# Layer 0's bias: sign passes, two more folds and an added row per key in place of the last matrix product

## The chip, the cores and the metric

The kernel runs on one core of a Trainium2 chip. A core has four compute engines that run side by side, each through its own instructions in order: TensorE (PE, matrix products, with a separate row PEld for its weight loads), VectorE (DVE), ScalarE (ACT) and GpSimd (POOL). SyncE (SP) computes nothing here; it issues DMA transfers in order and waits, in its queue, for what they need. All transfers share 16 DMA engines. The metric is the time of one execution on the device in microseconds, the median of three.

## What is computed

Four layers run one after the other on x (2 x 512 x 32 x 32); the change touches layer 0 alone. Layer 0 is an attention with 16 units (2 images x 8 heads). Each unit has 1024 queries and only 64 keys, sampled from the image at learned places. To the similarity comes a bias that is a small network of the distance between a query and a key:

```python
pos = grid_q[:, :, None, :] - grid_kv[:, None, :, :]
bias = jnp.sign(pos) * jnp.log1p(jnp.abs(pos))
bias = jax.nn.relu(bias @ cpb_w1 + cpb_b1)          # 2 -> 128
bias = jax.nn.relu(bias @ cpb_w2 + cpb_b2)          # 128 -> 128
bias = (bias @ cpb_w3 + cpb_b3).reshape(b, GROUPS, H * W, Hd * Wd)
sim = jnp.einsum('bhid,bhjd->bhij', qh, kh) + bias
attn = jax.nn.softmax(sim, axis=-1)
out = jnp.einsum('bhij,bhjd->bhid', attn, vh)
```

It has 128 hidden values for each of 16 x 64 x 1024 pairs of a key and a query, and this network is most of layer 0.

## The kernel before

**Steps.** `layer0` walks over `quads`, (u, o, half): 16 units u, eight groups o of eight keys, two halves of four keys. One such step is "step 2 o + half" of its unit, 0 to 15. For each step `first_hidden` makes h1, the first hidden layer of four keys, on DVE (L726), one step ahead: four 128 x 1024 halves in tiles of which two steps' worth exist. `second_hidden` (from L736) then runs the second layer for the four keys in four quarters q of 32 hidden channels: 32 matrix products of 128 x 32 by 512 columns (L752; each is two records in the trace) into hp, a PSUM tile of 4 keys x 32 channels by 1024 queries. There are three such tiles.

**The last layer without a product.** The magnitudes of `cpb_w3` are folded into the second layer and its channels are sorted by sign, so what is left is a sum of 128 values with signs. ACT does Relu on each quarter (L763) and a sign pass on quarter 0 (L767). Then y1 += y0 is an accumulating DMA from POOL (L772), y3 += y2 a POOL addition (L776), and one step later `join` does y3 += y1 on POOL (L779). In six steps of two units, the `fused` ones, DVE does Relu and y3 += y2 in one instruction (L761) and POOL's L776 is left out.

**Folds.** The 32 rows of a key are then folded on themselves by accumulating DMAs from POOL: 128 to 64 rows in `join` (L782), to 32 and to 16 in `refold` (L804, L807), 256 KB and 128 KB at the last two. Two DMAs on SP (L811) then gather the 16 rows of each half, four a key, into `sum` tiles: 128 rows for 32 keys. A tuple in `self.refolds` says when: the folds at the joins of steps i + 2 and i + 3, the gather at the end of step i + 4. `refold_more` works through that list.

**Last product.** In the next unit, at the end of step 5, `sum_product` (L819) adds the four rows of each key, with their signs, into `sim` (PSUM, one bank) by four products with a signed 0/1 matrix, `thrice`. `attend` for unit v = u - 1 follows: keys by queries into the same `sim` (L845), then softmax on DVE and ACT, one part a step, and the products with the values.

**Tables.** The logs of the distances come from DRAM: `table` has a 512 KB load (lb, on SP, L478) for every two groups, called at the start of an odd-numbered step. `send` ties it behind the last gather issued so far (`self.gathered`), in SP's order. POOL makes the table tx from it (L666), tied behind the last addition or fold issued (`self.added`), and DVE makes h1 from tx.

**Order.** The order of instructions on PE, ACT, DVE and POOL is as the program is written (`manual_schedule`); SP's is set by a scheduler within the ties above. `front` is a list of generators that prepare the next pair of units (normed input, queries, offsets, logs, sampled keys), `after` one with `attend` and the output projection. Each step takes one part of `after`, and one of `front` if that part said it was small.

Of the kernel before, what the change touches and what calls it, by code (L numbers as in the profile page):

```python
# [11 lines left out]
F32 = mybir.dt.float32  # L12
# [22 lines left out]
    ("cpb_w1", 2), ("cpb_b1", 1), ("cpb_b2", 1), ("cpb_w3", 1), ("cpb_b3", 1),  # L35
    ("index", 1), ("row", 1), ("shares", 4),
    ("gamma1", 1), ("vb1", CT),
# [20 lines left out]
class Net:  # L58
# [40 lines left out]
    def layer0(self):  # L99
# [3 lines left out]
        with ExitStack() as ctx:  # L103
# [45 lines left out]
            with self.tc.manual_schedule(engines=engines):  # L149
# [40 lines left out]
                for i, (u, o, half) in enumerate(quads):  # L190
# [23 lines left out]
                    if half == 1 and not last_set:  # L214
                        self.refolds.append((i + 2, i + (3 if u == last else 4), self.refold(group[-1][2], sums[o % 2], o // 2, u == last)))
                    if half == 1 and o == 2 and u > 0:
                        v = u - 1
                        sims[v] = ps_s.tile([P, HF], F32, tag="sim", name=f"sim{v}")
                        self.sum_product(sims[v], self.thrice, True, before)
                        if v == 8:  # L220
                            self.advance(after, lambda: False)
                            att = [apool.tile([P, N], F32, tag=f"att{t}", name=f"att{v}_{t}") for t in range(CT)]
                        self.advance(front, lambda: "v" in pairs[v // 2])
                        after.append(self.attend(v, pairs[v // 2], sims[v], att, ps))
                        if v % 8 == 7:
# [18 lines left out]
                self.single_product(u, o, 1, group[3][1], sims)  # L244
                sim = sims.pop(u)
                for n, _ in enumerate(self.attend(u, pairs[u // 2], sim, att, None)):
                    for _ in range({0: 5, 6: 1}.get(n, 0)):
                        next(share)
# [25 lines left out]
    def sorted_weights(self, keep):  # L274
# [43 lines left out]
        signed = keep.tile([P, N_SUMS], F32, tag="signed", name="signed")  # L318
        pool.tensor_scalar(signed, self.places[:, P:], c["sign"], 1.0, ALU.mult, ALU.mult)
        self.thrice, at = signed[:, 0:N_THRICE], N_THRICE  # L320
# [17 lines left out]
        nc.scalar.copy(self.magb, small)  # L338
        self.under = keep.tile([P, 1], F32, tag="under", name="under")
        pool.tensor_scalar(self.under, self.magb[:, 3, 0:1], -1.0, 1.0, ALU.mult, ALU.mult)  # L340
        self.flip = keep.tile([P, 1], F32, tag="flip", name="flip")
# [395 lines left out]
    def second_hidden(self, i, u, o, half, h1, one, final, last_set):  # L737
# [5 lines left out]
        vec, pool = nc.vector, nc.gpsimd  # L743
        fused = half == 1 and u > 0 and o in ((1, 3), (1, 2, 5, 6))[u % 2] and not final
        ys = []
        for q in range(4):
            hp = self.ps_h.tile([P, N], F32, tag="ps", name=f"hp_{u}_{o}{half}{q}")
            for h in range(2):
                cut = slice(h * HF, (h + 1) * HF)
                for k in range(4):  # L750
                    rows = slice(32 * k, 32 * k + 32)
                    nc.tensor.matmul(  # L752
                        hp[rows, cut], lhsT=self.l0w2[:, 32 * q : 32 * q + 32], rhs=h1[k][:, cut], start=True, stop=True
                    )
            if q < 3:
                y = self.hid2.tile([P, N], F32, tag=f"h2{q}", bufs=(2, 3, 2)[q], name=f"h2_{u}_{o}{half}{q}")
            else:
                y = one[half]
            ys.append(y)
            if q == 3 and fused:  # L760
                vec.scalar_tensor_tensor(y, hp, self.under, ys[2], ALU.max, ALU.add)  # L761
                continue
            nc.scalar.activation(y, hp, AF.Relu, bias=self.magb[:, q, 0:1])  # L763
            if q == 0 and fused:
                nc.scalar.activation(y, y, AF.Identity, scale=self.flip, bias=self.magb[:, 3, 0:1])
            elif q == 0:
                nc.scalar.activation(y, y, AF.Copy, scale=self.flip)  # L767
            elif q == 1:
                if final:
                    vec.tensor_tensor(y, y, ys[0], ALU.add)  # L770
                else:
                    self.added = pool.dma_start(y, ys[0], accum_op=ALU.add)  # L772
                if self.join:
                    self.join(final, i)
            elif q == 3:
                self.added = (vec if final else pool).tensor_tensor(y, y, ys[2], ALU.add)  # L776
# [11 lines left out]
    def refold_more(self, i, gather=False):  # L788

        going = []  # L790
        for at, last, fold in self.refolds:
            if at <= i and gather == (at == last):
                for _ in fold:
                    going.append((at + 1, last, fold))
                    break
            else:
                going.append((at, last, fold))
        self.refolds = going

    def refold(self, both, to, c, once):  # L800
# [7 lines left out]
        yield  # L808
        n = 4 if once else 8
        for half in range(2):  # L810
            self.gathered = nc.sync.dma_start(to[2 * c + half :: n, :], both[0::n, half, :])  # L811

# [24 lines left out]

    def attend(self, u, m, sim, att, ps):
        nc = self.nc
        g = u % 8  # L840
        rows = slice((g % 2) * DH, (g % 2 + 1) * DH)
        for h in range(2):
            for jj in range(2):
                at = h * NJ + jj * 32
                nc.tensor.matmul(  # L845
                    sim[at : at + 32, :],
                    lhsT=m["k"][:, g % 2, jj * 32 : jj * 32 + 32],
                    rhs=m["q"][:, 1 + 16 * h : 17 + 16 * h, 1 : 1 + W],
                    start=False,
                    stop=True,  # L850
                )
        yield
        t = self.soft.tile([P, 2 * NB, W], F32, tag="t", name=f"t{u}")
# [1217 lines left out]
def _places():  # L2071
# [5 lines left out]
    at = P  # L2077
    for keys, n in ((8, N_THRICE), (4, N_TWICE), (2, N_FOLDED), (1, N_SINGLE)):
        got[p, at + n - 32 + 4 * (p % keys) + p // 32] = 1
        at += n  # L2080
# [3 lines left out]
def _layout(i):  # L2084
# [10 lines left out]
    def over(v):  # L2095
# [12 lines left out]
        "index": np.arange(P, dtype=np.float32).reshape(P, 1),  # L2108
        "row": (np.arange(P) % 32 // 8).astype(np.float32).reshape(P, 1), "shares": over(np.arange(24, 108, 24, dtype=np.float32)),
        "gamma1": over(l1["gamma"]), "vb1": _per_partition(l1["bv"]),  # L2110
# [45 lines left out]
```

## Time and profile before

| | |
|---|---|
| median of three runs | 3213.95 us (3212.49 to 3214.47) |
| the profiled execution | 3214.26 us |
| its span, from first to last instruction | 3212.5 us, 58859 instructions |
| granted TensorE clock | 1.000 |
| layer 0 (until the first product of the block after it) | 0 to 1925.6 us |
| PE / DVE / ACT / POOL busy, share of the span | 99% / 76% / 60% / 73% |

The costliest groups of layer 0, with the count, the busy time in all and the mean of one:

| line, engine | what | count | us | ns each |
|---|---|---|---|---|
| L752 PE | second hidden layer, hp | 16384 | 1781.4 | 592 |
| L726 DVE | h1 | 1028 | 1181.1 | 1212 |
| L763 ACT | Relu | 978 | 1079.8 | 1110 |
| L779 POOL | y3 += y1 | 254 | 767.3 | 3021 |
| L776 POOL | y3 += y2 | 209 | 672.0 | 3215 |
| L772 POOL | issue of y1 += y0 | 255 | 354.6 | 1391 |
| L767 ACT | sign pass of quarter 0 | 210 | 241.8 | 1152 |
| L761 DVE | Relu and y3 += y2 in one | 46 | 59.1 | 1284 |
| L819 PE | last product | 128 | 18.8 | 592 |

A matrix product's mean of 592 ns is longer than its share of the time, since four of them run at once in different columns of the array: 16384 records fill 1781 us. POOL's times include overlap with the DMA instruction ahead of it. "Idle before" and "waited for" count the time an engine stood until the named instruction released it. Times in a timeline are in microseconds from the start of the span.

### The profile page before, as it was taken

The numbers are of one execution on the slowest core, as the hardware profiler recorded it, in microseconds if no ns is written. First come the engines' busy times: TensorE is split into PE (matmuls) and PEld (weight loads), VectorE is DVE, ScalarE is ACT, GpSimd is POOL, SyncE is SP. The second block draws the span as 40 slices with busy tenths as digits, with TensorE's granted clock in tenths as the row PEclk, the third lists the DMA queues.
The fourth block names the chain that finished last, engine by engine and source line by source line (L and its number), as shares of the span: only waits on it lengthen the run. The fifth ranks groups of instructions, "written<-read, shape, count | busy, mean of one in ns | idle before, by whom it ended". The sixth has DMA issues, their size and how long they took to land.

```text
span 3212.5 us, 58859 instructions
## 1 busy us (share of the span) xinstructions
PE 3194.7 (99%) x24068; PEld 1221.5 (38%) x24068; DVE 2425.7 (76%) x2792; ACT 1913.0 (60%) x1986; POOL 2340.5 (73%) x1633
## 2 busy tenths in 40 slices
PE   9999999999999999999999999999999999999999
PEld 4333333323333333333333334444556433455333
DVE  7788888888887677888877766475475689755897
ACT  7877887787786577787887742111221566113662
POOL 7998999999998679989999954342343458534575
PEclk9999999999999999999999999999999999999999
DMA  6888888898888578888888861110000000000001
GB/s 166 169 172 163 163 176 161 170 176 157 170 168 161 114 146 169 170 167 158 170 169 168 166 163 75 40 44 35 1 1 25 16 1 2 15 1 14 1 1 54
DMA packets 94349, 341.90 MB, mean 106 GB/s; under 512 B 18544, under 2 KB 20720, under 8 KB 76976
## 3 DMA queue, kind: packets, MB, share of 16 engines
q0 software_dynamic: 56672, 248.55, 41.9%
q1 hardware_dynamic: 36384, 87.33, 9.1%
q8 instruction: 194, 3.18, 0.4%
q10 hardware_dynamic: 1008, 2.10, 0.2%
q14 instruction: 91, 0.75, 0.1%
HBM read 67.37 MB, written 4.46 MB: 22 GB/s over the span
## 4 chain that ended last, share of the span: by engine, by line
PE 91%; DVE 5%; DMA 1%; POOL 1%; issue 1%; ACT 1%; DVEq 0%; POOLq 0%; ACTq 0%; SPq 0%
PE hp L752 53%; PE s L1692 5%; PE o L1721 5%; PE qk30P L1467 2%; PE qk20P L1467 2%; PE m_7P L976 1%; PE m_5P L976 1%; PE m_3P L976 1%; PE m_2P L976 1%; PE m_0P L976 1%; PE qk31P L1467 1%; PE qk21P L1467 1%; PE m_6P L976 1%; PE m_4P L976 1%; PE m_1P L976 1%; DVE sum L1708 1%
## 5 line engine op out<-in xcount | busy, mean ns | idle before, releaser
L752 PE MATMUL hp<-h,w2s 128*32 128x512 f32 x16384 | 1781.4, 592 | 2.8 <-ACT h L763 2.5
L726 DVE CUSTOM_DVE_ANT_1 h<-tx,bank 128x1024 f32<-128x1024 f32 (+1 forms) x1028 | 1181.1, 1212 | 170.3 <-PE hp L752 108.3
L763 ACT ACTIVATE h<-hp,magb 128x1024 f32<-128x1024 f32 x978 | 1079.8, 1110 | 360.9 <-PE hp L752 337.8
L752 PEld LDWEIGHTS hp<-h,w2s 128*32 128x32 f32 x16384 | 564.9, 110 | 1184.1 <-issue 1106.9
L779 POOL TENSOR_TENSOR h<-h,h 128x1024 f32<-128x1024 f32 x254 | 767.3, 3021 | 7.4 <-DMA h<-h 6.8
L776 POOL TENSOR_TENSOR h<-h,h 128x1024 f32<-128x1024 f32 x209 | 672.0, 3215 | 1.5 <-ACT h L763 1.5
L772 POOL DMA_DIRECT2D h<-h x255 | 354.6, 1391 | 130.5 <-ACT h L763 122.7
L1696 ACT ACTIVATE e<-s 128x1024 f32<-128x1024 f32 x256 | 262.0, 1025 | 181.0 <-PE s L1692 175.1
L1721 PE MATMUL o<-e,v 64*64 64x512 f32 x2048 | 265.3, 589 | 2.2 <-DVE q L1760 2.2
L1692 PE MATMUL s<-q,k 64*64 64x512 f32 x2048 | 266.0, 591 | 0.0
L767 ACT ACTIVATE h<-h,flip 128x1024 f32<-128x1024 f32 x210 | 241.8, 1152 | 6.9
L804 POOL DMA_DIRECT2D h<-h x124 | 197.5, 1593 | 0.2 <-issue 0.2
L1703 POOL TENSOR_TENSOR some<-some,e 128x1024 f32<-128x1024 f32 x64 | 167.7, 2620 | 26.7 <-ACT e L1696 23.9
L1701 POOL TENSOR_TENSOR some<-e,e 128x1024 f32<-128x1024 f32 x32 | 76.1, 2378 | 141.4 <-DVE sum L1710 106.3
L782 POOL DMA_DIRECT2D h<-h x127 | 158.3, 1247 | 4.6 <-issue 2.5
L807 POOL DMA_DIRECT2D h<-h x120 | 138.2, 1152 | 18.9 <-DMA h<-h 18.3
L1708 DVE TENSOR_TENSOR sum<-sum,e 128x1024 f32<-128x1024 f32 x64 | 124.0, 1937 | 29.5 <-ACT e L1696 26.8
L946 POOL TENSOR_TENSOR mlp_w<-mlp_w 128x512 f32<-128x512 f32 x16 | 23.9, 1493 | 160.1 <-DMA mlp_w<-in_mlp_w 114.7
L1721 PEld LDWEIGHTS o<-e,v 64*64 64x64 f32 x2048 | 77.9, 133 | 145.0 <-issue 135.1
L761 DVE SCALAR_TENSOR_TENSOR h<-hp,under,h 128x1024 f32<-128x1024 f32 x46 | 59.1, 1284 | 96.9 <-ACT h L763 70.9
L1692 PEld LDWEIGHTS s<-q,k 64*64 64x64 f32 x2048 | 76.6, 133 | 133.1 <-issue 117.2
L1042 ACT ACTIVATE mh<-mh,cols 128x512 f32<-128x512 f32 x64 | 46.1, 721 | 124.3 <-DVE mh L1060 64.3
(587 smaller groups left out, 3446.1 us busy)
## 6 DMA issues: line engine op xcount, KB each, us to landing
h<-h POOLq DMA_DIRECT2D x382, 512.0 KB, 5.8
lb<-logs SPq DMA_DIRECT2D x63, 512.0 KB, 7.2
h<-h POOLq DMA_DIRECT2D x124, 256.0 KB, 5.0
mlp_w<-in_mlp_w SPq DMA_DIRECT2D x16, 1024.0 KB, 4.8
h<-h POOLq DMA_DIRECT2D x120, 128.0 KB, 3.8
sum<-h SPq DMA_DIRECT2D x240, 64.0 KB, 3.0
x<-in_x SPq DMA_DIRECT2D x8, 512.0 KB, 7.6
qkw<-in_l_qk SPq DMA_DIRECT2D x2, 2048.0 KB, 7.9
```

The source lines that it names most:

```text
L726: self.nc.vector._custom_dve(TENSOR_ADD_SAT, out=h1[r][:, k, cut, :], in0=x[:, 4 * half + 2 * r + k, :].unsqueeze(1).to_broadcast([P, H // ...
L752: nc.tensor.matmul(hp[rows, cut], lhsT=self.l0w2[:, 32 * q : 32 * q + 32], rhs=h1[k][:, cut], start=True, stop=True)
L763: nc.scalar.activation(y, hp, AF.Relu, bias=self.magb[:, q, 0:1])
L767: nc.scalar.activation(y, y, AF.Copy, scale=self.flip)
L772: self.added = pool.dma_start(y, ys[0], accum_op=ALU.add)
L776: self.added = (vec if final else pool).tensor_tensor(y, y, ys[2], ALU.add)
L779: (vec if final else pool).tensor_tensor(z, z, other, ALU.add)
L804: nc.gpsimd.dma_start(both[0::4], both[2::4], accum_op=ALU.add)
L976: self.nc.tensor.matmul(acc[p], lhsT=w[:, a, k, p * P : (p + 1) * P], rhs=right(r, k), start=k == 0, stop=k == 1)
L1692: nc.tensor.matmul(s[halves[c], par, :], lhsT=ks[p][rows, at : at + DH], rhs=qs[p][rows, cut], start=True, stop=True)
L1696: nc.scalar.activation(e, s, AF.Exp, scale=DH**-0.5)
L1721: nc.tensor.matmul(o[halves[par], r, :], lhsT=v[n // 2][rows, n % 2, at : at + DH], rhs=e[rows, par, :], start=(n == 0), stop=(n == NB - 1),)
```

## The change

For units v = 0 to 13 the last product goes. In its place, one unit later:

- at the end of step 3 (for the first of the two sum tiles) and step 5 (for the second), ACT multiplies the sum tile by its signs in place (`last_sign`, one per row);
- `keys_rows` folds the tile twice more by accumulating DMAs from POOL, 128 rows to 64 (256 KB) and to 32 (128 KB), at the joins two and three steps later, and two DMAs on SP copy the 32 rows, one a key, into a tile `rows` of 128 x 512 at the end of that third step;
- keys by queries now start the sum in `sim` (`keys_queries`, still after step 5), and `attend`, which begins at step 10 instead of step 5, adds `rows` to `sim` on DVE.

So that four rows of a key lie side by side, the gathers write 16 adjacent rows instead of every eighth, and `thrice`, still used by unit 14, has another pattern. The tuple of `refolds` has a third number, the step from which the gather may go. The `rows` tile has the tag and the one buffer of `pt`, the turned weights of the softmax.

The fused steps change too. `late` is the old form (Relu and y3 += y2 on DVE), now at o = 1, 2 of even units and o = 1, 2, 3, 4 of odd ones (before: 1, 3 and 1, 2, 5, 6). `early` is new, at o = 0 and 7 of units 1 to 14: Relu of quarter 2 and y2 += y0 in one instruction on DVE, with neither ACT's Relu of quarter 2 nor the DMA y1 += y0.

```diff
@@ layer0, in the loop over quads
                     if half == 1 and not last_set:
-                        self.refolds.append((i + 2, i + (3 if u == last else 4), self.refold(group[-1][2], sums[o % 2], o // 2, u == last)))
-                    if half == 1 and o == 2 and u > 0:
-                        v = u - 1
+                        end = i + (3 if u == last else 4)
+                        self.refolds.append((i + 2, end, end, self.refold(group[-1][2], sums[o % 2], o // 2, u == last)))
+                    v = u - 1
+                    if half == 1 and o in (1, 2) and 0 <= v < last - 1:
+                        z = before[o - 1]
+                        if o == 1:
+                            rows = self.soft.tile([P, HF], F32, tag="pt", name=f"rows{v}")
+                        nc.scalar.activation(z, z, AF.Copy, scale=self.last_sign)
+                        self.refolds.append((i + 2, i + 4, i + 3, self.keys_rows(z, rows, o - 1)))
+                    if half == 1 and o == 2 and v >= 0:
                         sims[v] = ps_s.tile([P, HF], F32, tag="sim", name=f"sim{v}")
-                        self.sum_product(sims[v], self.thrice, True, before)
+                        if v == last - 1:
+                            self.sum_product(sims[v], self.thrice, True, before)
+                        self.advance(front, lambda: "v" in pairs[v // 2])
+                        self.keys_queries(v, pairs[v // 2], sims[v], v < last - 1)
+                    if v >= 0 and (o, half) == ((5, 0) if v < last - 1 else (2, 1)):
...
-                        self.advance(front, lambda: "v" in pairs[v // 2])
-                        after.append(self.attend(v, pairs[v // 2], sims[v], att, ps))
+                        after.append(self.attend(v, pairs[v // 2], sims[v], att, ps, rows if v < last - 1 else None))
@@ second_hidden
-        fused = half == 1 and u > 0 and o in ((1, 3), (1, 2, 5, 6))[u % 2] and not final
+        late = half == 1 and u > 0 and o in ((1, 2), (1, 2, 3, 4))[u % 2]
+        early = half == 1 and 0 < u < 2 * BP - 1 and o in (0, 7)
...
-            if q == 3 and fused:
-                vec.scalar_tensor_tensor(y, hp, self.under, ys[2], ALU.max, ALU.add)
+            if q == 3 and late:
+                vec.scalar_tensor_tensor(y, hp, self.under[:, 1:2], ys[2], ALU.max, ALU.add)
+                continue
+            if q == 2 and early:
+                vec.scalar_tensor_tensor(y, hp, self.under[:, 0:1], ys[0], ALU.max, ALU.add)
                 continue
             nc.scalar.activation(y, hp, AF.Relu, bias=self.magb[:, q, 0:1])
-            if q == 0 and fused:
-                nc.scalar.activation(y, y, AF.Identity, scale=self.flip, bias=self.magb[:, 3, 0:1])
+            if q == 0 and (late or early):
+                at = 3 if late else 2
+                nc.scalar.activation(y, y, AF.Identity, scale=self.flip, bias=self.magb[:, at, 0:1])
...
-                else:
+                elif not early:
                     self.added = pool.dma_start(y, ys[0], accum_op=ALU.add)
@@ refold_more
-        for at, last, fold in self.refolds:
-            if at <= i and gather == (at == last):
+        for at, last, when, fold in self.refolds:
+            if at < last and at <= i and not gather or at == last and when <= i and gather:
@@ refold
-        n = 4 if once else 8
         for half in range(2):
-            self.gathered = nc.sync.dma_start(to[2 * c + half :: n, :], both[0::n, half, :])
+            at = 2 * c + half
+            if once:
+                self.gathered = nc.sync.dma_start(to[at::4, :], both[0::4, half, :])
+            else:
+                self.gathered = nc.sync.dma_start(to[16 * at : 16 * at + 16, :], both[0::8, half, :])
+
+    def keys_rows(self, z, to, jj):
+
+        nc = self.nc
+        nc.gpsimd.dma_start(z[0::2], z[1::2], accum_op=ALU.add)
+        yield
+        nc.gpsimd.dma_start(z[0::4], z[2::4], accum_op=ALU.add)
+        yield
+        for h in range(2):
+            at = h * NJ + jj * 32
+            self.gathered = nc.sync.dma_start(to[at : at + 32, :], z[0::4, h * HF : (h + 1) * HF])
@@ attend
+        if bias is not None:
+            nc.vector.tensor_tensor(sim, sim, bias, ALU.add)
         t = self.soft.tile([P, 2 * NB, W], F32, tag="t", name=f"t{u}")
```

The rest of the diff makes the signs of the sum tiles' rows at the start (a column `last_row`, a few one-column instructions on POOL) and moves keys by queries out of `attend` into `keys_queries`.

More of the change, by code (lines that the diff above doesn't have):

```diff
@@ L35 @@
     ("cpb_w1", 2), ("cpb_b1", 1), ("cpb_b2", 1), ("cpb_w3", 1), ("cpb_b3", 1),
-    ("index", 1), ("row", 1), ("shares", 4),
+    ("index", 1), ("row", 1), ("last_row", 1), ("shares", 4),
     ("gamma1", 1), ("vb1", CT),
@@ L245, in layer0 @@
                 sim = sims.pop(u)
+                self.keys_queries(u, pairs[u // 2], sim, False)
                 for n, _ in enumerate(self.attend(u, pairs[u // 2], sim, att, None)):
@@ L318, in sorted_weights @@
         signed = keep.tile([P, N_SUMS], F32, tag="signed", name="signed")
-        pool.tensor_scalar(signed, self.places[:, P:], c["sign"], 1.0, ALU.mult, ALU.mult)
+        self.last_sign = keep.tile([P, 1], F32, tag="last_sign", name="last_sign")
+        pool.tensor_scalar(self.last_sign, self.col("last_row"), c["groups"], 2.0, ALU.is_lt, ALU.mult)
+        pool.tensor_scalar(self.last_sign, self.last_sign, -1.0, 1.0, ALU.add, ALU.mult)
+        for cut, sign in ((slice(0, N_THRICE), self.last_sign), (slice(N_THRICE, N_SUMS), c["sign"])):
+            pool.tensor_scalar(signed[:, cut], self.places[:, P:][:, cut], sign, 1.0, ALU.mult, ALU.mult)
         self.thrice, at = signed[:, 0:N_THRICE], N_THRICE
@@ L338, in sorted_weights @@
         nc.scalar.copy(self.magb, small)
-        self.under = keep.tile([P, 1], F32, tag="under", name="under")
-        pool.tensor_scalar(self.under, self.magb[:, 3, 0:1], -1.0, 1.0, ALU.mult, ALU.mult)
+        self.under = keep.tile([P, 2], F32, tag="under", name="under")
+        pool.tensor_scalar(self.under, self.magb[:, 2:4, 0], -1.0, 1.0, ALU.mult, ALU.mult)
         self.flip = keep.tile([P, 1], F32, tag="flip", name="flip")
@@ L790, in refold_more @@
         going = []
-        for at, last, fold in self.refolds:
-            if at <= i and gather == (at == last):
+        for at, last, when, fold in self.refolds:
+            if at < last and at <= i and not gather or at == last and when <= i and gather:
                 for _ in fold:
-                    going.append((at + 1, last, fold))
+                    going.append((at + 1, last, when, fold))
                     break
             else:
-                going.append((at, last, fold))
+                going.append((at, last, when, fold))
         self.refolds = going
@@ L836, in single_product, with keys_queries, attend @@
             )
-    def attend(self, u, m, sim, att, ps):
+    def keys_queries(self, u, m, sim, start):
+        for h in range(2):
+            for jj in range(2):
+                at = h * NJ + jj * 32
+                self.nc.tensor.matmul(
+                    sim[at : at + 32, :],
+                    lhsT=m["k"][:, u % 2, jj * 32 : jj * 32 + 32],
+                    rhs=m["q"][:, 1 + 16 * h : 17 + 16 * h, 1 : 1 + W],
+                    start=start,
+                    stop=True,
+                )
+    def attend(self, u, m, sim, att, ps, bias=None):
         nc = self.nc
@@ L841, in attend @@
         rows = slice((g % 2) * DH, (g % 2 + 1) * DH)
[L842 to L852, printed above, removed]
+        if bias is not None:
+            nc.vector.tensor_tensor(sim, sim, bias, ALU.add)
         t = self.soft.tile([P, 2 * NB, W], F32, tag="t", name=f"t{u}")
@@ L2077, in _places @@
     at = P
-    for keys, n in ((8, N_THRICE), (4, N_TWICE), (2, N_FOLDED), (1, N_SINGLE)):
+    got[p, at + p // 4] = 1
+    at += N_THRICE
+    for keys, n in ((4, N_TWICE), (2, N_FOLDED), (1, N_SINGLE)):
         got[p, at + n - 32 + 4 * (p % keys) + p // 32] = 1
@@ L2108, in _layout @@
         "index": np.arange(P, dtype=np.float32).reshape(P, 1),
-        "row": (np.arange(P) % 32 // 8).astype(np.float32).reshape(P, 1), "shares": over(np.arange(24, 108, 24, dtype=np.float32)),
+        "row": (np.arange(P) % 32 // 8).astype(np.float32).reshape(P, 1),
+        "last_row": (np.arange(P) % 4).astype(np.float32).reshape(P, 1), "shares": over(np.arange(24, 108, 24, dtype=np.float32)),
         "gamma1": over(l1["gamma"]), "vb1": _per_partition(l1["bv"]),
```

## The prediction

> **What bounds the kernel now.** I read the page first, then the chain of waits in layer 0, the busy time by window, the waits of each engine, and last the timeline of GpSimd (POOL) and of the SP queue.
>
> The chain of waits, a stretch of unit 4, and the window of about one unit:
> ```profile
> 624.22 13.87 PE hp L752 x128
> 638.09 0.86 PE sim L819 x8
> 638.94 0.86 PE sim L845 x8
> 639.80 41.20 PE hp L752 x384
> ...
> 535.00:649.00 114.00, 114.00 (x1064) 38.94 (x1060) 97.80 (x108) 90.83 (x90) 106.63 (x79) 1.00 0.86 167
> ```
> TensorE (PE) has no gap: a step of 64 hp records takes 13.87/2 = 6.9 us, one after the other. A unit of 16 steps takes about 114.2 us. The columns of the window line are PE, PEld, DVE, ACT, POOL: POOL is at 106.6 of 114, so it is the second bound, close behind. Its waits over 137 to 936 us, seven units:
> ```profile
> POOL h L772 <- ACT h L763: 36.9, 21, 4.2
> POOL h L807 <- DMA h<-h: 10.6, 10, 2.2
> ...
> POOL h L772 <- DMA h<-h: 1.5, 2, 0.8
> ```
> Only the wait for ACT is real slack (POOL has caught up). The same question over 1200 to 1756 us gives 20.9, 6.6 and 6.0. Over these 1355 us the ACT wait comes to 57.8/1355 x 114.2 = 4.9 us a unit.
>
> POOL's timeline, with the SP queue, and the landing times:
> ```profile
> 575.50 3.16 POOL L779 TENSOR_TENSOR h<-h,h 128x1024 f32<-128x1024 f32 x1
> 578.33 1.06 POOL L807 DMA_DIRECT2D h<-h  x1
> 578.96 1.34 POOL L782 DMA_DIRECT2D h<-h  x1
> 579.54 3.19 POOL L776 TENSOR_TENSOR h<-h,h 128x1024 f32<-128x1024 f32 x1
> 581.93 1.53 POOL L666 TENSOR_SCALAR tx<-lb,cols 128x512 f32<-128x512 f32 x1
> ...
> 581.76 16.49 SPq L811 DMA_DIRECT2D sum<-h  x4
> 598.34 0.53 SPq L478 DMA_DIRECT2D lb<-logs  x1
> ...
> lb<-logs SPq DMA_DIRECT2D x63, 512.0 KB, 7.2
> h<-h POOLq DMA_DIRECT2D x120, 128.0 KB, 3.8
> ```
> The shown spans overlap, so I take each end less the end before it: L807 costs POOL 0.73 us (579.39 - 578.66), L782 0.91, L776 2.43, tx 0.73; elsewhere L772 gives 0.84 and L804 0.80. The gather on SP starts 581.76 - 578.33 = 3.4 us after its fold L807, and lb is issued right behind a gather. In the kernel before that costs nothing: the lb of 569.69 is used by the tx of 581.93, 12.2 us later.
>
> One place shows what a late lb does (unit 9 to 10, where logs were made late):
> ```profile
> 1178.88 3.18 POOL L776 TENSOR_TENSOR h<-h,h 128x1024 f32<-128x1024 f32 x1
> 1193.13 0.77 POOL L666 TENSOR_SCALAR tx<-lb,cols 128x512 f32<-128x512 f32 x1 [11.06 <-DMA lb<-logs]
> ...
> 1199.57 1.92 PE L752 MATMUL hp<-h,w2s 128*32 128x512 f32 x16 [2.24 <-ACT h L763]
> ```
> POOL stood 11.06 us behind the tx, everything queued after it (the fold L772, then the sums) was late, ACT could not reuse its tiles, and PE stopped for 2.24 us and then 0.26: POOL can fall some 8 us behind before PE stops.
>
> **What the skill says.** The Trainium skill, "DMA: Bandwidth & Descriptors", section "SWDGE vs HWDGE vs iDMA": accumulating DMAs can be issued from GpSimd alone, whose cores compute the descriptors; the trace agrees (0.7 to 0.9 us of POOL each). The same page, "Two DMAs through the same engine are not ordered": the engine that issues a dependent DMA must wait for the first one's semaphore. SP does so: its L811 rows wait for the folds. "Perfetto Trace Analysis", section "DMA Instruction — SWDGE (GPSIMD)": the shown end is that of descriptor generation, not of the data; hence 3.8 us to landing for an instruction shown as about 1.1.
>
> **The change part by part.**
>
> *Product removed.* 14 units x 0.86 us (the eight sim L819 records) = 12.0 us off PE. Keys by queries stay (0.86 us, only earlier in order).
>
> *ScalarE.* Signs add 2 passes a unit at about 1.15 us (as L767); the two early folds remove two L763 at 1.11. The late ones move to o = 1, 2, so that a sign pass takes the place of a missing Relu: 5 passes a step, as before. Nothing, hidden by 114 - 91 us. The signs need gathers issued two steps before, as the product did.
>
> *VectorE.* Added a unit: 2 x 1.28 us (as L761) and one 128x512 add at 0.69 (as L867), 3.3 us; 97.8 + 3.3 stays under 113. But DVE can make the h1 of step i+2 only after PE ends step i, and needs 4.6 of the 6.9 us. After step 5 of units 2, 4, 6 and 8 the late add (1.28) now stands with the normed input (L539, median 2.35): 1.28 + 2.35 + 4.62 + about 0.2 = 8.4 against 6.9 + 0.86 of PE: 0.7 us x 4 = 2.8 us, if PE is otherwise the bound. In unit 10 this collision goes.
>
> *Front moved.* attend starts five steps later, so the next pair's offsets run ahead: in unit 9 logs come two steps before lb needs them, and the 2.24 + 0.26 = 2.5 us above go.
>
> *GpSimd issues.* Four new folds: 2 x 0.80 (as L804) + 2 x 0.74 (as L807), about 3.2 with the wider ones a little dearer; two L772 go, 1.7. Net +1.5 us a unit. The bytes stay: 2 x 512 KB go, 2 x (256 + 128) and 4 x 64 KB come, so the DMA share stays near 0.86.
>
> *Gather layout.* 16 adjacent rows instead of every eighth: between nothing and a few tenths of their 3.0 us either way; two steps of slack cover it. I take nothing. The sum tiles (three buffers) are held longer, but a buffer is refilled only after the rows left it, by order on SP; the rows tile shares pt's buffer, free since step 15. Nothing.
>
> *SP queue and the new wait: the dear one.* The rows of the second z are issued at the end of step 8 (its "when" is i + 3, the very step of its second fold); the load lb(u,3) is called at the start of step 9 and tied behind the last gather. So SP holds lb until that fold has landed. On POOL, between the fold and the tx of this lb stand only L782 and L776. This holds in the built order of units 1 to 14. From the fold's issue: 3.4 us to the rows, 1.3 for their two issues (gather pairs took 1.1 to 1.7), 7.2 to lb's landing = 11.9. POOL gets to tx after 0.74 + 0.91 + 2.43 = 4.1. It then stands 7.8 us, in every unit, and however late it runs, since both ends hang on the same fold. Behind it stand L772 and all later sums; ACT waits for their tiles, PE for ACT. With lb at its fastest (5.0) the wait is 5.6, at its slowest (9.2) 9.8.
>
> *Sum.* POOL's slack: 4.9, plus 0.5 (L772's own waits for a DMA, 7.5 us in 1355 rounded down) plus 0.6 (my share of L807's waits, 1.5 us a unit, that a new fold in between covers), less 1.5 for issues, less 0.9 because PE's unit gets shorter: 3.6 us. Each unit is thus longer than PE's by 7.8 - 3.6 = 4.2 us. Units 1 and 9 start without a debt (the projection, 28 us of PE alone, now stands at the head of unit 9) and cost 1.5 each, an estimate below the 2.5 of the 11 us wait. 12 x 4.2 + 2 x 1.5 = 53.4; less 12.0 and 2.5: +38.9 us. The profiled execution took 3214.26 (span 3212.5), against a median of 3213.95: 3253.
>
> **Rivals.**
>
> B, the wait is absorbed and PE stays the bound: -12.0 - 2.5 + 2.8 = -11.7, 3203. For it: no gap on PE, one 11 us wait cost only 2.5. Against: it came once, with two late adds behind it to catch up; fourteen of them don't fit in 3.6 us a unit. It decides where the wait at this tx is under 3.6 us; the time equals the one before at (14.5 - 3)/12 + 3.6 = 4.6. With lb never seen under 5.0 us that needs most of the fold's landing hidden too.
>
> C, the wait is there but smaller and POOL has more slack, so that gain and loss nearly cancel: wait 5.6 and slack 4.7 give 12 x 0.9 + 3 - 14.5 = -0.7, 3214. For it: POOL's slack is the softest number here.
>
> D, the wait is real but VectorE becomes late too: after step 10 the add, the transpose and maxima (3.7 us) stand before h1, with 2.05 us of slack a step; if that adds 0.5 us a unit, 3260. It lies inside A's range.
>
> That the change doesn't do what it says I can exclude: the order of instructions has the products gone and the rows added in 14 units.
>
> **How the numbers follow.** A (with D) 0.72, B 0.20, C 0.08. The likeliest is A: 3253. Its own range: wait 5.6, excess 2.0, 24 + 1.5 - 14.5 = +11, 3225; wait 9.8, excess 6.2, 74.4 + 5 - 14.5 = +65, 3279. A measurement tells 0.2% (6.4 us) from no change. To leave out at most 2 in 10 the range must reach B's centre: 3203 to 3280. Slower 0.73 (A and a little of C), same 0.07, faster 0.20.
>
> **What would show it.** Right: POOL's tx waits for DMA lb<-logs 14 times, 5 to 10 us each (14.6 us in all before); PE hp gets idle, mostly behind ACT or DVE, in step 10 to 12 of each unit; sim<-sum only in two units of PE; the idle at 1199 gone. Wrong: those waits under 4 us, or PE still without a gap in units 2 to 8, or the loss found on DVE after L539.

## The result and the profile after

| | before | changed |
|---|---|---|
| median (lowest to highest, runs) | 3213.33 us (3211.27 to 3214.47, 6) | 3291.17 us (3289.57 to 3293.18, 6) |
| span of the profiled execution | 3212.5 us | 3288.3 us |
| ratio, 95% interval | | 1.0243 (1.023 to 1.0256) |

The change makes the kernel 77.8 us slower. The direction was forecast, the size was not: 38.9 us were expected and the range ended at 3280.

The loss lies in layer 0. Take a unit from its keys by queries (after step 5) to those of the next unit; the first interval begins in unit 1. The fourteen intervals, in us, with two kernels of the experiments beside them (x4 does without the product, x8 is the last repaired version):

```
before   115.3 114.1 114.4 114.1 114.4 114.1 115.5 142.6 119.7 117.4 115.5 114.1 115.6 112.3   sum 1639
changed  115.6 122.6 122.6 119.0 120.9 118.7 124.6 146.7 121.0 118.4 121.8 119.3 122.3 122.0   sum 1716
x4       114.4 113.2 113.5 113.3 113.5 113.2 114.7 141.7 120.3 115.8 114.8 113.2 114.7 112.3   sum 1629
x8       114.8 113.4 115.5 114.9 113.1 114.8 114.2 143.4 113.1 117.2 114.9 114.8 114.3 115.6   sum 1634
```

The changed kernel loses in all but the first interval, up to 9.7 us in one. From the page of the changed kernel, the chain and three groups (busy time, mean of one, then the idle time before them and what ended it):

```profile
PE 63%; POOL 16%; DVE 9%; DMA 6%; issue 4%; ACT 1%; SPq 0%; DVEq 0%; POOLq 0%; ACTq 0%
...
L768 PE MATMUL hp<-h,w2s 128*32 128x512 f32 x16384 | 1816.7, 597 | 53.5 <-ACT h L782 47.9
...
L792 POOL DMA_DIRECT2D h<-h x227 | 333.8, 1471 | 73.0 <-ACT h L782 64.6
...
L681 POOL TENSOR_SCALAR tx<-lb,cols 128x512 f32<-128x512 f32 x63 | 78.4, 1245 | 108.9 <-DMA lb<-logs 72.5
```

PE was 91% of the chain and is 63%. It stands 53.5 us ahead of hp (2.8 before). POOL stands 108.9 us ahead of tx (14.6 before), where the prediction put the dear wait. POOL also still stands 64.6 us for ACT: its slack is not used up although it is what is late. A stall is passed on to ACT and PE within a step or two, as shown next; the slack comes at other times, when POOL has caught up and waits for ACT's next result.

One such stall, in unit 4. First SP's queue, then POOL, then ACT, then PE, each from its own timeline of the changed kernel (start, duration, what, and in brackets the idle time before it with what ended that):

```profile
571.25 1.56 SPq L845 DMA_DIRECT2D rows<-sum  x2
572.86 0.58 SPq L493 DMA_DIRECT2D lb<-logs  x1
```
```profile
565.82 1.93 POOL L841 DMA_DIRECT2D sum<-sum  x1
566.42 2.22 POOL L802 DMA_DIRECT2D h<-h  x1
566.99 4.09 POOL L796 TENSOR_TENSOR h<-h,h 128x1024 f32<-128x1024 f32 x1
578.46 0.77 POOL L681 TENSOR_SCALAR tx<-lb,cols 128x512 f32<-128x512 f32 x1 [7.39 <-DVE bank L897]
579.18 0.86 POOL L792 DMA_DIRECT2D h<-h  x1
```
```profile
583.64 1.11 ACT L782 ACTIVATE h<-hp,magb 128x1024 f32<-128x1024 f32 x1 [5.32 <-DMA h<-h]
```
```profile
584.81 15.39 PE L768 MATMUL hp<-h,w2s 128*32 128x512 f32 x128 [2.48 <-ACT h L782]
```

The rows go out 3.5 us after the issue of their fold ends (565.82 + 1.93 = 567.75), the load of logs right behind them, and tx starts 5.6 us after that load's issue. The timeline names a small copy of DVE as the releaser, which is no input of tx; a wait for several semaphores is put down to the last one seen. The load itself landed 5.4 us after its issue, 0.2 us before tx starts, and x1 and x3 below show that it is what POOL stood for. Behind tx stands the transfer y1 += y0 of L792: ACT waits 5.32 us for a tile that it frees, and PE 2.48 us for ACT. So a wait of 7.39 us stopped PE here, where the prediction read from one place of the kernel before that POOL can fall some 8 us behind.

The gap costs PE more than its length. Windows of the changed kernel around it (length, then PE, PEld, DVE, ACT, POOL busy; then granted clock, DMA share, GB/s):

```profile
582.00:585.00 3.00, 0.52 (x5) 0.19 (x8) 3.00 (x4) 1.32 (x2) 3.00 (x3) 0.90 0.76 153
585.00:592.00 7.00, 7.00 (x56) 1.80 (x54) 5.06 (x5) 5.93 (x6) 7.00 (x6) 0.80 0.63 115
592.00:600.00 8.00, 8.00 (x80) 2.05 (x68) 6.24 (x7) 4.42 (x6) 8.00 (x7) 1.00 1.03 215
```

After the gap the clock is 0.80 on the mean of 7 us, and 56 records of products go through where 65 do at full clock (6.9 us a step of 64). The 128 records that took 13.87 us before take 15.39. The Trainium skill, "TensorE: Matmul & The Clock Gate", section 'Part 1: The HAM clock gate (the "warmup" mystery)', says that the clock halves after an idle stretch of about 3.4 us and comes back after a busy one; the trace agrees in kind, in windows of 2 us the clock reads 0.50 just after such a gap, but not in the length: this gap of PE was 2.48 us. Over all windows of 2 us from 137 to 1756 us, PE's busy time times (1 - clock) adds up to 11.9 us in the changed kernel, and to 0 in the kernel before. The clock fell at seven gaps: four stand behind the load (343.41, 584.81, 1068.42 and 1576.77 us), two behind a gather (448.58 and 928.28, see below), one behind DVE (1683.71).

The waits in the same stretch, the changed kernel (us in total, times, longest):

```profile
ACT h L782 <- DMA h<-h: 79.8, 36, 6.8
POOL tx L681 <- DMA lb<-logs: 66.1, 10, 8.6
...
ACT h L782 <- DMA sum<-h: 40.7, 24, 4.5
DVE sampling L604 <- DMA at<-spots: 36.0, 4, 10.5
...
PEld hp L768 <- DVE h L741: 27.9, 50, 1.0
```

The first two belong together, as shown. The next two, ACT for a gather and DVE for the sampling places, are new as well (4.9 us each before) and stood in no sum of the prediction. They were the rivals for what was left.

Both can be seen in unit 3, before its load of logs is issued. SP, then ACT and PE, then DVE:

```profile
434.52 1.13 SPq L845 DMA_DIRECT2D rows<-sum  x2
439.52 1.16 SPq L834 DMA_DIRECT2D sum<-h  x2
441.11 0.65 SPq L493 DMA_DIRECT2D at<-spots  x1
```
```profile
447.41 2.12 ACT L782 ACTIVATE h<-hp,magb 128x1024 f32<-128x1024 f32 x2 [8.73 <-DMA sum<-sum]
448.58 1.08 PE L768 MATMUL hp<-h,w2s 128*32 128x512 f32 x4 [5.90 <-ACT h L782]
```
```profile
447.75 1.22 DVE L604 TENSOR_TENSOR sampling<-at,bank 128x1024 f32<-128x1024 f32 x1 [9.48 <-DMA at<-spots]
```

The rows of the first tile land at 439.45 us, and the gather follows at once. In all 14 units the gather is issued within 0.4 us of that landing. Its second half lands at 447.30, and ACT, which needs the tile that this gather reads, starts 0.1 us later (the fold `sum<-sum` that the timeline names lands only at 448.6). The places are loaded behind the gather, and DVE stands for them. PE stands 12.3 us behind such gathers in four units (3, 5, 7 and 11), of 46.3 us in front of hp in this stretch.

### The profile page after: what moved, and what is told of

It reads as the page before. It is cut to its first block, busy times and chain, and to the rows that moved or that the text cites. A ratio compares the mean times of both kernels' runs of the same rounds, so it can differ in the third digit from the quotient of the medians.

```text
span 3288.3 us, 58784 instructions
## 1 busy us (share of the span) xinstructions
PE 3217.4 (98%) x23956; PEld 1210.3 (37%) x23956; DVE 2470.8 (75%) x2834; ACT 1905.2 (58%) x1985; POOL 2362.1 (72%) x1664
## 4 chain that ended last, share of the span: by engine, by line
PE 63%; POOL 16%; DVE 9%; DMA 6%; issue 4%; ACT 1%; SPq 0%; DVEq 0%; POOLq 0%; ACTq 0%
PE hp L768 26%; POOL h L799 7%; PE s L1730 5%; PE o L1759 5%; DMA h<-h 3%; POOL h L796 3%; DVE h L741 3%; POOL h L792 2%; PE qk20P L1505 1%; PE qk30P L1505 1%; PE m_0P L1014 1%; PE m_7P L1014 1%; PE m_5P L1014 1%; PE m_4P L1014 1%; PE m_2P L1014 1%
## 5 line engine op out<-in xcount | busy, mean ns | idle before, releaser
L768 PE MATMUL hp<-h,w2s 128*32 128x512 f32 x16384 | 1816.7, 597 | 53.5 <-ACT h L782 47.9
L782 ACT ACTIVATE h<-hp,magb 128x1024 f32<-128x1024 f32 x950 | 1043.1, 1108 | 470.9 <-PE hp L768 306.5
L799 POOL TENSOR_TENSOR h<-h,h 128x1024 f32<-128x1024 f32 x254 | 750.5, 2955 | 14.0 <-DMA h<-h 11.8
L796 POOL TENSOR_TENSOR h<-h,h 128x1024 f32<-128x1024 f32 x209 | 661.9, 3167 | 5.1 <-ACT h L782 5.1
L792 POOL DMA_DIRECT2D h<-h x227 | 333.8, 1471 | 73.0 <-ACT h L782 64.6
L787 ACT ACTIVATE h<-h,flip 128x1024 f32<-128x1024 f32 x182 | 209.6, 1152 | 6.0
L1741 POOL TENSOR_TENSOR some<-some,e 128x1024 f32<-128x1024 f32 x64 | 167.6, 2619 | 26.6 <-ACT e L1734 24.1
L802 POOL DMA_DIRECT2D h<-h x127 | 173.1, 1363 | 6.1 <-issue 4.0
L824 POOL DMA_DIRECT2D h<-h x124 | 168.3, 1358 | 7.6 <-DMA h<-h 5.1
L827 POOL DMA_DIRECT2D h<-h x120 | 148.7, 1239 | 17.0 <-DMA h<-h 16.8
L681 POOL TENSOR_SCALAR tx<-lb,cols 128x512 f32<-128x512 f32 x63 | 78.4, 1245 | 108.9 <-DMA lb<-logs 72.5
```

Of the source, the lines that this page charges most:

```text
L768: nc.tensor.matmul(hp[rows, cut], lhsT=self.l0w2[:, 32 * q : 32 * q + 32], rhs=h1[k][:, cut], start=True, stop=True)
L799: (vec if final else pool).tensor_tensor(z, z, other, ALU.add)
L802: pool.dma_start(one[2][0::2], one[2][1::2], accum_op=ALU.add)
L824: nc.gpsimd.dma_start(both[0::4], both[2::4], accum_op=ALU.add)
```

## The experiments

Each run is compared with runs of the kernel before on the same chip, whose medians lay between 3213.09 and 3214.55 us. All kernels but x4, x11 and x14 do the whole computation.

| run | what | median, us | ratio (95%) |
|---|---|---|---|
| x1 | rows of both tiles a step later | 3246.27 | 1.0104 (1.0088 to 1.0121) |
| x2 | rows of the second tile alone later | 3247.04 | 1.0109 (1.0092 to 1.0126) |
| x3 | rows of the first tile alone later | 3288.84 | 1.0235 (1.0218 to 1.0252) |
| x4 | before, without the product | 3200.53 | 0.9962 (0.9948 to 0.9976) |
| x5 | x1 + fourth sum buffer | 3240.42 | 1.0075 (1.0056 to 1.0093) |
| x6 | x5 without early folds | 3247.78 | 1.0105 (1.0084 to 1.0127) |
| x7 | x5 + sampling later | 3234.67 | 1.0077 (1.0059 to 1.0095) |
| x8 | x7 + attend one step later | 3208.43 | 0.9983 (0.9976 to 0.999) |
| x9 | changed + attend one step later | 3290.53 | 1.024 (1.0223 to 1.0257) |
| x10 | x1 + attend one step later | 3236.20 | 1.0064 (1.0048 to 1.0081) |
| x11 | x4 + attend where the change has it | 3201.52 | 0.996 (0.9946 to 0.9974) |
| x12 | x8 with three sum buffers | 3243.05 | 1.0095 (1.0078 to 1.0112) |
| x13 | x8 with the sampling not later | 3219.50 | 1.0021 (1.0014 to 1.0029) |
| x14 | x7 without the add of the rows | 3208.03 | 0.9984 (0.9977 to 0.999) |
| x15 | x7 without early folds | 3243.77 | 1.009 (1.0073 to 1.0107) |

**The load behind the rows: x1, x2, x3.** The edit of x1; x2 has `i + 2 + o` and x3 `i + 5 - o` in its place:

```diff
-                        self.refolds.append((i + 2, i + 4, i + 3, self.keys_rows(z, rows, o - 1)))
+                        self.refolds.append((i + 2, i + 4, i + 4, self.keys_rows(z, rows, o - 1)))
```

> The rows of both sum tiles are issued one step later, at the end of steps 7 and 9 (when is i + 4), so that SP issues the load lb(u,3), and the stores of logs and spots, ahead of the rows that come after them in the program. Theory T1 (the load held behind the rows is the loss): the waits of tx for lb fall from 109 us to under 20 us and the time to 3203 to 3212. Theory T2 (a good part of the loss is the front moved ahead, DVE standing at the sampling for the at load, and the collisions of late adds on DVE): 3225 to 3250, with the waits of DVE for at<-spots still near 36 us. Theory T3 (POOL is simply out of slack with four more issues a unit): over 3230, with PE idle behind ACT and no waits at tx.

> Only the rows of the second sum tile are issued one step later (end of step 9 instead of 8); those of the first stay at the end of step 6. T1: nearly the whole gain of the run with both late, 3205 to 3215, waits at tx gone. T2: the logs and spots of odd units still go behind the rows of the first tile, DVE still stands some 36 us at the sampling, and the time stays 10 to 25 us above the run with both late.

> Only the rows of the first sum tile are issued one step later (end of step 7 instead of 6); those of the second stay at the end of step 8, with lb behind them. T1: no gain, 3283 to 3293, waits at tx still about 109 us. T2: the waits of DVE for at<-spots fall under 10 us and the time by 10 to 25 us, to 3265 to 3282.

With the second tile's rows out of the load's way 44.1 us go (x2), with both 44.9 (x1), with the first alone 2.3 (x3). The idle time ahead of tx falls from 108.9 us to 11.1 (x2) and 4.5 (x1), and stays at 107.7 in x3. So the dear wait of the prediction is real, is tied to the second tile as it said, and taking it away in this manner brings 44 us.

Both T1 and T2 missed in x1 and x2. T1 had the times 30 us and more too low. T2 had x1's time, but not its waits: DVE's wait for the places is 2.3 us in x1, not 36; it is 25.1 in x2, and yet the two take the same time. In x3 it fell to 9.5 us and brought next to nothing, with the load's stall still there. T3, POOL out of slack, fits the times too, but not the trace: with the load out of the way POOL stands for ACT's results as long as before, 110.7 us in x2 against 99.1 over the same stretch.

The gain is a net one, for the edit brings a wait of its own. The rows of the second tile now leave one step ahead of the add instead of two. The add in the changed kernel and in x2, over 137 to 1756 us (busy, mean | idle before):

```profile
L890 DVE TENSOR_TENSOR sim<-sim,rows 128x512 f32<-128x512 f32 x13 | 9.0, 690 | 0.3 <-DMA rows<-sum 0.3
```
```profile
L890 DVE TENSOR_TENSOR sim<-sim,rows 128x512 f32<-128x512 f32 x13 | 9.0, 695 | 11.8 <-DMA rows<-sum 8.3 <-issue 3.5
```

The lost clock, by the sum above, falls with the gaps too: from 11.9 us to 5.0 in x1 and 0 in x2. What the load's wait alone costs these runs do not tell.

**The product: x4.** `sum_product` is called for unit 14 alone, and keys by queries start the sum; the bias of units 0 to 13 is left out.

> The kernel before, with the last product left out for units 0 to 13 and nothing in its place: these units' similarity is without the bias. This is the gain of the removed product by itself. All theories: 14 x 0.86 = 12.0 us, 3201 to 3202. If POOL is already as much of a bound as PE, less: 3204 to 3210.

12.8 us go. Between x1 and x4 45.7 us are left to be explained. In x2, as much is left (46.5), and there PE stands only 4.8 us in front of hp in the stretch, none of it behind the gathers: it is its weight loads that stand for h1, 44.3 us against 9.8 before. So DVE is late.

**Sum buffers: x5, and the early folds: x6.** The fourth buffer needs 4 KB a partition, found by putting small tiles into parts of others:

```diff
-        return self.hid2.tile([P, N], F32, tag="sum", bufs=3, name=name)
+        return self.hid2.tile([P, N], F32, tag="sum", bufs=4, name=name)
...
-        spots = self.fone.tile([P, 2 * NJ, 2], F32, tag="spots", name=f"at{b}{t}")
+        spots = m["at"]
...
-        wx = self.fone.tile([P, 2 * NJ], F32, tag="wx", name=f"wx{b}{t}")
+        more = self.fone.tile([P, N], F32, tag="xn", name=f"wx{b}{t}")
```

x6 has `early = False` beside it.

> The rows of both tiles late, as in x1_rows_late (3246.27 us), and in addition a fourth buffer for the sum tiles (room for it made by putting three small tiles into parts of others, with the same work). Theory T2, the sum buffers: what x1 still loses comes mostly from a sum tile held until its rows are read, so that the gather into the next tile of that tag waits on SP for the rows' transfer and comes late to ScalarE's Relu; then ScalarE's waits for DMA sum<-h (23.4 us over 137 to 1756 us in x1) fall under 6, and the time to 3215, between 3205 and 3228. Theory T3, VectorE's and GpSimd's additions (two more STT, one add, four folds less two a unit): the time stays within 8 us of x1's, 3238 to 3252, with TensorE waiting behind ScalarE all the same.

> x5_late_four without the two early folds of VectorE a unit (steps 1 and 15 go back to GpSimd's accumulating transfer). GpSimd issues two more transfers a unit, 1.7 us, and VectorE does 2.6 us less. If GpSimd is what is short beside the waits (T2), it gets slower than x5, by 5 to 20 us; if VectorE's early folds are what costs (T3), it gets faster than x5 by 5 to 25 us.

ACT's waits for the gathers went as expected (23.4 us to 2.5), but the time fell by 5.9 us only: T2 missed here. T3 in the form "the early folds cost" falls too, since without them it did not get faster (7.4 us slower, with ranges that overlap). The odd units up to 7 stayed long in x5 (117.8 to 121.2), and DVE's timeline of x5 in unit 5 showed why, with h1 standing behind the sampling; SP's queue is put ahead of it:

```profile
664.88 2.97 SPq L848 DMA_DIRECT2D rows<-sum  x2
667.95 0.98 SPq L494 DMA_DIRECT2D sampling<-spots  x1
```
```profile
675.46 1.22 DVE L605 TENSOR_TENSOR sampling<-sampling,bank 128x1024 f32<-128x1024 f32 x1 [8.11 <-DMA sampling<-spots]
```

Before, the places were loaded at 666.97 us and used at 686.85, 20 us later, because attend's steps came in between. Attend now begins five steps later, and load and use are neighbours. That alone does not make DVE stand: in x11 below, attend begins as late, the places are loaded at 651.51 us and used at 656.92, and DVE stood 0.03 us. In x5 the load goes out right behind the rows, when DVE has already been standing for 0.6 us. How much of the delay is the rows and how much the place of the load in the program was not told apart.

**The sampling: x7, and attend's place: x8.**

```diff
         xnT = m["xT"]
         yield
+        if bt:
+            yield
```
```diff
-                    if v >= 0 and (o, half) == ((5, 0) if v < last - 1 else (2, 1)):
+                    if v >= 0 and (o, half) == ((5, 1) if v < last - 1 else (2, 1)):
```

> x5_late_four (3240.42 us) with one idle turn more between the load of the sampling places and VectorE's first use of them, so that the use comes one to two steps later, behind the late fold of step 11. Theory T4, the front moved: with attend five steps later, the next pair's places are stored, loaded and used within two steps (20 us apart before), VectorE stands up to 8.1 us for them in the odd units, h1 is late and TensorE waits; then the intervals of the odd units (117.8 to 121.3 us in x5) fall to 117 or less, and the time to 3222, between 3212 and 3232. Theory T3, VectorE is simply too full there: the odd units stay within 1 us of x5 and the time between 3234 and 3246.

> x7_sampled_later with attend, which begins with VectorE's add of the rows, one step later (after step 11 in place of step 10). Theory T5: VectorE waits for the second tile's rows at the add (13.6 us in seven units of x5), because the rows are issued only one step ahead; then that wait goes under 3 us and the time falls 6 to 14 us below x7. If the add's wait lies in slack that VectorE has anyway, the time stays within 5 us of x7.

x7 lies 5.8 us under x5, with ranges that overlap (3231.59 to 3244.49 and 3233.46 to 3245.49): not resolved as such, outside T4's 3212 to 3232 and just inside T3's range. The odd units did come down, to between 116.1 and 117.3 in units 1 to 7. x8 falls by 26.2 us, twice what T5 expected, and is faster than the kernel before, by 0.17%. The group of the add, from x7 and then from x8 over 137 to 1756 us (busy, mean | idle before):

```profile
L895 DVE TENSOR_TENSOR sim<-sim,rows 128x512 f32<-128x512 f32 x13 | 9.1, 697 | 15.6 <-issue 9.2 <-DMA rows<-sum 6.3
```
```profile
L895 DVE TENSOR_TENSOR sim<-sim,rows 128x512 f32<-128x512 f32 x14 | 9.7, 692 | 0.0
```

Of the 15.6 us the trace puts 6.3 down to the rows; for 9.2 it shows no releaser. And the waits of PE's weight loads for h1 in the two, x7 and then x8:

```profile
PEld hp L773 <- DVE h L746: 39.8, 72, 1.0
```
```profile
PEld hp L773 <- DVE h L746: 19.2, 47, 1.0
```

A step later the rows have landed, DVE does not stand at the add, and PE waits half as long for h1. Attend's six steps are where DVE has least to spare: in x7 it is busy for 29.8 of 31.0 us from 798.5, with PE at four and a half steps in that time. What it loses there it can hardly make up.

**What adds up and what does not: x9, x10, x11.**

> The changed kernel with one edit: attend and its add of the rows begin one step later (after step 11). The load of logs stays behind the second tile's rows. If the two costs add (load 44 us, attend's place 26 us), 3265, between 3255 and 3275; if the load's stall covers the other, it stays at 3291 within 8 us.

> x1_rows_late (3246.27 us; both tiles' rows a step later) with attend one step later, three buffers for the sum tiles and the sampling as in the changed kernel. If attend's place is what costs (T5, 26 us from x7 to x8), 3220, between 3212 and 3228; what is left against x8 (3208.43 us) is the price of the third buffer and the early sampling. If x8's gain needs the fourth buffer and the later sampling, it stays above 3232.

> x4_before_no_product (3200.53 us; the bias of units 0 to 13 left out) with attend five steps later and the late folds at o = 1, 2 or 1 to 4, as the change places them, and nothing else of the change: no signs, no rows, no new folds, no early folds. It is left out: the bias of units 0 to 13. If attend's place with the sampling two steps behind its load is dear by itself, 3200.5 + 20 to 35, that is 3220 to 3235; if it costs only together with the rows, the add and the early folds of VectorE, 3198 to 3208.

In x9 the same edit that gave 26 us to x7 gives 0.6. The expectation put that down to the load's stall, which is still there (111.1 us ahead of tx); but the changed kernel also has no wait at the add to lose, 0.3 us as shown, and these runs do not tell the two reasons apart. In x10 the edit gives 10.1, a miss against 3220; at 3236.20 it lies where x8's gain was said to need the fourth buffer and the later sampling. x11 (bias of units 0 to 13 left out) has the two moves of the change in the kernel x4 and nothing else of it:

```diff
-                        after.append(self.attend(v, pairs[v // 2], sims[v], att, ps))
+                        going = self.attend(v, pairs[v // 2], sims[v], att, ps)
+                        if v < last - 1:
+                            next(going)
+                    if u > 0 and (o, half) == ((5, 0) if u < last else (2, 1)):
+                        after.append(going)
...
-        fused = half == 1 and u > 0 and o in ((1, 3), (1, 2, 5, 6))[u % 2] and not final
+        fused = half == 1 and u > 0 and o in ((1, 2), (1, 2, 3, 4))[u % 2] and not final
```

It shows that attend's new place, with the late folds moved, costs next to nothing by itself, 1.0 us. It takes unit 9's interval from 120.3 to 113.4, the gain that the prediction claimed from earlier logs, and the other thirteen intervals lose 4.9 us together. The place is dear only with the rows.

**One taken from x8, or from x7: x12 to x15.** Each undoes one edit: `bufs=3`; the idle turn gone; the add of `bias` gone; `early = False`.

> x8_attend_later (3208.43 us) with three buffers for the sum tiles in place of four, nothing else. Theory T2: a sum tile is held until its rows are read, so that the gather into the next one waits on SP, ScalarE's Relu waits for its tile and TensorE for ScalarE (x10, with three buffers: 49.3 us of ScalarE waiting for DMA sum<-h); then this one loses 20 to 30 us and comes to 3233, between 3226 and 3242. If the buffer is worth the 6 us that x1 to x5 showed, 3210 to 3219.

> x8_attend_later without the idle turn between the load of the sampling places and their use (so x5_late_four with attend one step later). Theory T4 (VectorE stands for the places in the odd units): 3214 to 3222; if the later attend already took that wait away, within 4 us of x8, 3204 to 3213.

> x7_sampled_later (3234.67 us) without VectorE's add of the rows, so the bias of units 0 to 13 is left out; the rows are still moved. Theory T5a, the add and its wait for the rows are what makes VectorE late after step 10 (the burst of attend stands ahead of h1): 3212, between 3206 and 3220. Theory T5b, the two early folds of VectorE beside attend are: stays above 3226.

> x7_sampled_later (3234.67 us) without the two early folds of VectorE a unit (their sums go back to GpSimd's transfers). T5b: VectorE gets 2.6 us a unit back around attend, and the time falls to 3215 to 3226. T5a, or GpSimd too short of time: it stays above 3230 or rises, as from x5 to x6 (+7).

x12 is the clear one: three buffers instead of four cost 34.6 us, some more than the 20 to 30 expected. Its memory layout is that of x8, so it is the buffer. SP's queue of x12 in unit 3, then ACT, then PE:

```profile
429.78 1.80 SPq L850 DMA_DIRECT2D rows<-sum  x2
431.68 1.29 SPq L494 DMA_DIRECT2D sampling<-spots  x1
433.02 0.54 SPq L494 DMA_DIRECT2D lb<-logs  x1
435.36 10.66 SPq L839 DMA_DIRECT2D sum<-h  x4
```
```profile
442.94 2.12 ACT L787 ACTIVATE h<-hp,magb 128x1024 f32<-128x1024 f32 x2 [9.83 <-DMA sum<-h]
```
```profile
444.11 16.15 PE L773 MATMUL hp<-h,w2s 128*32 128x512 f32 x135 [7.00 <-ACT h L787]
```

And SP's queue of x8 at the same place:

```profile
424.63 1.46 SPq L839 DMA_DIRECT2D sum<-h  x2
426.26 2.91 SPq L850 DMA_DIRECT2D rows<-sum  x2
429.27 1.03 SPq L494 DMA_DIRECT2D sampling<-spots  x1
430.35 1.35 SPq L494 DMA_DIRECT2D lb<-logs  x1
```

With four buffers the gather goes ahead of the rows. With three it goes into the very tile that the rows are still read from, so it stands behind them and two loads, and is issued 0.15 us after they land (435.21). It also frees the tile that ACT writes next, so ACT stands 9.83 us and PE 7.00. SP is not among the engines whose order the kernel writes out (`engines` of `manual_schedule` has PE, ACT, DVE and POOL): its order follows from what a transfer must wait for, and a buffer less turned it round.

Where the sampling is not later, the fourth buffer is worth less: from x10 to x13, which differ in it and in the small tiles moved for it, 16.7 us. So its price is 5.9, 16.7 or 34.6 us, by what else is in the way. All three have the first tile's rows a step later than the changed kernel has them; there the same order stands in SP's queue (unit 3 above), but a fourth buffer was not tried.

x13: the later sampling is worth 11.1 us in x8 (T4, inside its 3214 to 3222). x14, with the bias of units 0 to 13 left out: without the add x7 falls by 26.6 us, which is about the add's busy and idle time in x7, 9.1 + 15.6 = 24.7 (T5a). x15: without the early folds x7 gets no faster (9.1 us slower, with ranges that overlap), so T5b falls.

## Why the prediction was right in direction and wrong in size

The sum was -12.0 - 2.5 + 53.4 = +38.9 us. Measured, it is -12.8 + 44.9 + 45.7 = +77.8: the product (x4), the load (x1), and what is left between x1 and x4. The step that failed is the one that put this last term at nothing, in three places: VectorE, the front, the sum tiles.

- *Product removed, 12.0.* Right: 12.8 (x4).
- *The dear wait.* Right in place and cause. The unit 4 wait was 7.39 us against 7.8, and the whole 108.9 us in 17 waits is 6.4 on the mean. Its cost was put at 53.4, and 44 to 45 go in x1 and x2. That the two are close is in part luck: the 44 are net of the wait that the edit brings to the add, and have lost clock in them that the prediction did not count.
- *VectorE.* Rival D was named, but given 0.5 us a unit, 7 in all, and kept inside A. Once the load is out of the way DVE is what is late (x2). From x7 to x8 26.2 us go, and the add with its wait costs 26.6/14 = 1.9 us a unit in x7 (x14). The average load, 97.8 of 114, hid that attend's six steps have almost no slack. The wait at the add itself is not the change's: it is 0.3 us there, and came with the later rows.
- *"Front moved"*, taken as a gain of 2.5 alone. The gain came in its place (6.9 us in unit 9's interval, x4 to x11) but not in the sum (x11 is 1.0 us slower than x4). And the places for the sampling came to lie next to their use, behind the rows on SP: DVE stood 36.0 us for them in the changed kernel, and loading them a turn ahead is worth 11.1 us in x8 (x13). The prediction did not name that.
- *"The sum tiles (three buffers) are held longer, but a buffer is refilled only after the rows left it, by order on SP ... Nothing."* It looked at the order for safety and not for who stands in the queue behind it. The refilling gather also frees ACT's next tile, and it was made to wait for the rows' landing. In the changed kernel PE stands 12.3 us behind it; taken away, the wait is worth 5.9 to 34.6 us (x1 to x5, x12 to x8), with the first tile's rows a step later than in the changed kernel.
- *TensorE's clock.* No step had it. 11.9 us of it are lost in the changed kernel after gaps of PE.
- *Signs, gather layout, four more folds, late folds moved, "nothing" or 1.5 us of POOL.* Right as a sum: x8 has them all and lies 7.9 us above x4, 0.6 us a unit, with the add's busy time of 0.69 among it.

These figures overlap and are not to be added. Against x4 the changed kernel loses 90.6 us: 44.9 go with the load (x1), and of the other 45.7 x8 recovers 37.8 by sum buffer, sampling and the add's place together. How those 45.7 divide in the changed kernel, where the first tile's rows leave a step earlier and the add does not wait, stays open: every one of x5 to x8 and x12 to x15 is built on x1. Rivals B and C, with the wait absorbed or small, are excluded by x1.

The late fold of DVE (Relu and y3 += y2 in one) beside the normed input (2.8 us in the prediction, "if PE is otherwise the bound") was not measured by itself; it lies within the 7.9 us.

x8 is the version to keep: 3208.43 us over 20 runs, 0.17% under the kernel before (0.10 to 0.24%), the change with four edits (rows later, a fourth buffer, sampling later, attend later), none to its arithmetic. x4 marks what the idea could bring at most, 3200.5.

## What to carry to other kernels

When a buffer's last reader moves later, find the transfer that refills it and ask what that refill itself frees, and what stands behind it in its queue: here a tile buffer counted as safe, and so as free, was worth up to 35 us. Slack is to be read in the steps where the work lands, not as an average: 16 us of DVE's 114 were idle, and in six steps almost none. Costs that lie in parallel hide each other, so undo the suspects from the best version as well as adding repairs to the worst: the fourth buffer showed 6 us one way and 35 the other. And look in the trace for what a repair brings: the rows that made way for the load made DVE wait at the add.

## What the hardware showed that was not expected

After some PE gaps in front of hp the granted clock fell to a half for the next few microseconds, so that a gap of 2.48 us was followed by 128 records in 15.39 us instead of 13.87. The length of the gap alone does not decide it. In the changed kernel all seven gaps of 2.48 us and more were followed by it, and none of the shorter ones. But in x12 a gap of 2.20 us (to 207.77) was followed by a clock of 0.50 from 208 to 211 us, and in x9 one of 3.23 us (to 1453.88) left it at 1.00. So no safe length can be given from these runs.
